# A second Strassen step for four of the seven products of V in layer 1 of two attention blocks

## The chip, the cores and the metric

The kernel runs on one core of one Trainium2 chip. The metric is the time of one execution on the device in microseconds; the median of three runs is given, and one execution was profiled.

## The reference

Two attention blocks follow each other on x of 8 images, 512 channels and 32 x 32 = 1024 positions, all in float32. Layer 0 has a group norm, 8 heads and a residual. Layer 1, which the change is about, normalises a whole image and has one head over all channels. Cut to what matters:

```python
n = (x - mean) * rsqrt(var + EPS) * gn_gamma + gn_beta      # mean, var over an image
q, k, v = wq @ n + bq, wk @ n + bk, wv @ n + bv             # 512 x 512 weights, 1024 positions
attn = softmax(q.T @ k * c ** -0.5)                         # 1024 x 1024
x = x + wo @ (v @ attn.T) + bo
```

## The kernel before

The program is unrolled over the 8 images. For each one it runs `layer0` (V, the last q and k, attention by pairs of heads, the projection, and at its end the first q and k of the next image) and then `attention1` (q, V, scores, values). The orders of TensorE, ScalarE and VectorE are those in which the program is written (`manual_schedule`). The DMA queue of SyncE (SP below) and GpSimd (POOL) are ordered by the framework, which also adds the waits.

**Folded weights.** Layer 1 multiplies wq with wk and wv with wo once, at the start. So `attention1` makes one product for q (`wqk1`), uses x itself in the place of k, and one product for V (`wvo1`), after whose use in the values no projection is left. V here means `wvo1` times x.

**Strassen.** Nearly every product is done in Winograd's form of Strassen's scheme: the two operands are cut into quarters A11 to A22 and B11 to B22, and seven products of quarters and of their sums S1 to S4 and T1 to T4 replace eight. Three of the seven, A11 B11, S2 T2 and S3 T3, are summed up one after the other in one bank of PSUM, together with A22 T4 (the generator `strassen` calls it `line`); ScalarE copies the running sum out after each of the first three, and VectorE adds the other bank (`single`) to the copies.

**Layer 1's V before** is `make_v` at L648 for both halves of the positions, with the products in `by_positions` at L617. A product of quarters has 4 matmul calls for each half: two blocks of 128 positions are the stationary operand, the 256 channels of the weight are the moving one, and 256 input channels are summed in two calls. In the profile a call leaves two records of TensorE (PE) and two of its weight load (PEld), here and everywhere.

**The second step** is there already in two places. The scores of layer 1 take it for four products in `twice` (L1267), with halves made by `halve_a` and `halve_b`. Layer 0's q and k take it in `by_two_steps` (L513): the products in `PAIRS`, namely A12 B21, S1 T1, S4 B22 and A22 T4, are each cut once more into seven, and two of them share a bank. The generator `pair(n)` makes one step for each of the seven inner products; the generator `line(i)` makes the three products that keep one step, and adds them to what the pairs left. `together` goes round its generators, one step each, so `pair(0)` and `pair(1)` alternate for 14 steps and `line(0)` and `line(1)` for 6. `WeightTwice` (L483) holds the inner sums of a weight's four parts: it makes them once, stores them in DRAM, and loads them for each image as two tiles of 512 KB.

**Order.** `at_steps(steps, {n: [...]})` runs the hooks of n after step n was issued. Because the engines take the order of the program, a hook's instructions stand on VectorE between the sums of step n and those of step n + 1. Before the change, `attention1` has these hooks:

```python
at_steps(together(make_q(0), make_q(1)), {..., 6: halve_b("T1"), 7: halve_b("B22"), ...})   # q
at_steps(together(*[make_v(...) for n2 in range(2)]), {                                      # V
    1: [finish_q], 4: [lambda: halve_a("S1")], 6: [lambda: halve_a("A12")],
    8: [lambda: halve_a("S4")],
})
at_steps(together(line(0), p5, line(1), p5), {})                                             # scores
at_steps(together(line(2), p2, line(3), p2), {..., 4: halve_a("A22"), 6: halve_b("T4"), ...})
```

`finish_q` makes S1 to S4 of q with `finish` (L187 to L190), four sums of 128x1024 at once. `halve_a` is L468 and `halve_b` L477 in the profile, four sums of 128x256 each.

**Buffers.** Nearly all tiles of 128x1024 come from one pool of 36 (`tile2`). PSUM has two tags, "s" and "o", with two tiles of two banks each. Weights rotate through three tiles; `next_weight` takes the next one and issues the load of the one after the next on SP's queue (L208).

Of the kernel before, what the change touches and what calls it, by code (L numbers as in the profile page):

```python
# [39 lines left out]
ALU = mybir.AluOpType  # L40
# [6 lines left out]
P = 128  # L47
# [3 lines left out]
NT = N // P  # L51
# [14 lines left out]
def two_attention_blocks(  # L66
# [34 lines left out]
    def tile2(name):  # L101
        return tpool.tile([P, 2, HALF], FP, tag="t", name=name)
# [80 lines left out]
        t = t.rearrange("p (a k o) -> p a k o", a=len(A_PARTS), o=width)  # L183
        return {a: t[:, n, :, :] for n, a in enumerate(A_PARTS)}

    def finish(parts, a21):
        nc.vector.tensor_tensor(parts["S1"], a21, parts["A22"], ALU.add)  # L187
        nc.vector.tensor_tensor(parts["S2"], parts["S1"], parts["A11"], ALU.subtract)
        nc.vector.tensor_tensor(parts["S3"], parts["A11"], a21, ALU.subtract)
        nc.vector.tensor_tensor(parts["S4"], parts["A12"], parts["S2"], ALU.subtract)  # L190

    W_SIZE = len(A_PARTS) * C
    stored = {}
# [65 lines left out]
    def next_weight():  # L259

        w = waiting.pop(0)
        if coming:
            name = coming.pop(0)
            waiting.append(Weight(name) if name in stored else load_first(name))
        return w
# [34 lines left out]
    class Norm:  # L300
# [54 lines left out]
        def bias(self):  # L355
            both, bias = self.tile("both"), self.tile("bias", NC)
            nc.vector.tensor_tensor(both, self.mean, self.rstd, ALU.mult)
            nc.vector.tensor_scalar(bias, made["v_g"], both, None, ALU.mult)
            nc.vector.tensor_tensor(bias, made["v_b"], bias, ALU.subtract)
            return bias  # L360
# [149 lines left out]
                    made[a] = q  # L510
            return made

    def by_two_steps(rows_of, twice_a, bs, twice_b, pairs, bias, name):  # L513

        def pair(n):
            line, single = (banks(tag, f"ps_{tag}{n}_{name}")[:, 0, :] for tag in "so")  # L520

            def multiply(bank, x, y, start):
                for i, (a, v) in enumerate(PAIRS[n]):
                    nc.tensor.matmul(  # L524
                        bank[:, i * 2 * P : (i + 1) * 2 * P], twice_a[a][x], twice_b[v][y],
                        start=start and i == 0, stop=True, skip_group_check=True,
                    )

            def at(r, t):
                return pairs[n][r][:, :, t * 2 * P : (t + 1) * 2 * P]  # L530

            def of(bank):
                return bank.rearrange("p (i q) -> p i q", i=2)

            def add(bank, r, t):
                nc.vector.tensor_tensor(at(r, t), of(bank), at(r, t), ALU.add)

            def take(bank, r, t):
                nc.scalar.copy(at(r, t), of(bank))

            for bank, x, y, start, use, r, t in [
                (line, "A11", "B11", True, take, 0, 0), (single, "A12", "B21", True, add, 0, 0),
                (line, "S2", "T2", False, take, 0, 1), (single, "S1", "T1", True, take, 1, 1),
                (line, "S3", "T3", False, add, 1, 1), (single, "S4", "B22", False, add, 0, 1),
                (line, "A22", "T4", False, take, 1, 0),
            ]:
                multiply(bank, x, y, start)
                use(bank, r, t)
                yield

        def line(i):
            bank = banks("o", f"ps_l{i}_{name}")[:, 0, :]

            def multiply(a, v, start):
                for k in range(2):
                    nc.tensor.matmul(  # L556
                        bank, rows_of(i, a)[:, k, :], bs[v][:, k, :], start=start and k == 0,
                        stop=k == 1, skip_group_check=True,
                    )

            def add(j, half, n):
                c = pairs[j][i][:, half, :]
                nc.vector.scalar_tensor_tensor(c, bank, bias(i, n), c, ALU.add, ALU.add)

            (c11, c22), (c12, _) = ([p[i][:, half, :] for half in range(2)] for p in pairs)
            nc.vector.tensor_tensor(c12, c12, c22, ALU.add)
            multiply("A11", "B11", True)
            add(0, 0, 0)
            yield
            multiply("S2", "T2", False)  # L570
            add(1, 0, 0)
            yield
            multiply("S3", "T3", False)
            add(0, 1, 1)
            add(1, 1, 1)
            yield

        yield from together(pair(0), pair(1))
        yield from together(line(0), line(1))

# [16 lines left out]
    def at_steps(steps, hooks):  # L597

        n = -1
        for n, _ in enumerate(steps):  # L600
            for hook in hooks.get(n, []):
                hook()
        assert n >= max(hooks, default=-1)
# [199 lines left out]
    def blank(n, name):  # L803
        return [tile2(f"{name}_{i}") for i in range(n)]

    def flat(t):
        return t.rearrange("p h n -> p (h n)")
# [15 lines left out]
    def pairs_qk_twice(w, twice_a, oc, bs, twice_b, qs, ks, b):  # L823

        pairs = [[tile2(f"{n}_{name}_0_{b}_{oc}") for name in "qk"] for n in ["c11", "c12"]]
        for i, ts in enumerate([qs, ks]):
            (c11, c22), (c12, c21) = ([p[i][:, half, :] for half in range(2)] for p in pairs)
            ts[oc], ts[oc + 2] = [c11, c12], [c21, c22]

        def bias(i, n):  # L830
            at = [V_BQ0, V_BK0][i] + oc + 2 * n
            return vec[:, at : at + 1]

        of = both_of(w)
        return by_two_steps(of, twice_a.all(of), bs, twice_b, pairs, bias, f"qk_0_{b}")

    ORDER = [0, 2, 1, 3]

# [321 lines left out]
    def attention1(xs, norm, b, at_values):  # L1160
# [9 lines left out]

        qs = quarters_of(f"q_1_{b}")
        w = next_weight().parts[0]
        combine, later = Combined(f"1_{b}"), []
        combine.take(xs)
        bs = combine.parts
# [8 lines left out]
        def halve_b(name):  # L1184
            twice_b[name] = quarters_b(bs[name], f"{name}_twice_{b}")

        def make_q(c):
# [24 lines left out]
            4: [norm.deviation, lambda: combine.make(4)],  # L1212
            6: [lambda: halve_b("T1")],
            7: [lambda: halve_b("B22")],
            5: [norm.untaken, lambda: later.pop(0)(), lambda: later.pop(0)()],
        })
        bias = norm.bias()
        vs = blank(NT // 2, f"v_1_{b}")
        w = next_weight().parts[0]
        (a11, a21), (a12, a22) = qs  # L1220
        q_parts = {"A11": a11, "A12": a12, "A22": a22}

        def finish_q():
            for i in range(1, 5):
                q_parts[f"S{i}"] = tile2(f"s{i}_q_{b}")
            finish(q_parts, a21)

        at_steps(together(*[make_v(w, n2, bs, vs, f"v_1_{b}") for n2 in range(2)]), {
            1: [finish_q], 4: [lambda: halve_a("S1")], 6: [lambda: halve_a("A12")],
            8: [lambda: halve_a("S4")],  # L1230
        })


# [97 lines left out]
        def c22(k):  # L1331
# [1 line left out]
            exp_of(ps[1][k][1])  # L1333

        p5 = twice("S1", "T1", "oo", 1, 1, True, False)
        at_steps(together(line(0), p5, line(1), p5), {})
        p2 = twice("A12", "B21", "oo", 0, 0, False, True)
        at_steps(together(line(2), p2, line(3), p2), {
            0: [lambda: with_p5(0, 1, 0)], 1: [lambda: c22(0)], 4: [lambda: halve_a("A22")],
            6: [lambda: halve_b("T4")], 8: [lambda: with_p5(0, 1, 1)], 10: [lambda: add_up(1, 0, 1)],  # L1340
        })
        at_steps(together(
            twice("S4", "B22", "so", 0, 1, False, True), twice("A22", "T4", "so", 1, 0, False, True)
# [1 line left out]

        tps = {f"T{n}": [tile2(f"t{n}_p_1_{b}_{k}") for k in range(2)] for n in range(1, 5)}
        svs = {f"S{n}": tile2(f"s{n}_v_1_{b}") for n in range(1, 5)}
        v_parts = [
            {
                "A11": vs[k][:, :, : 2 * P], "A12": vs[2 + k][:, :, : 2 * P],  # L1350
                "A22": vs[2 + k][:, :, 2 * P :],
                **{n: flat(t).rearrange("p (h u o) -> p h u o", h=2, u=2)[:, k] for n, t in svs.items()},
            }
            for k in range(2)
# [9 lines left out]
        def finish_values(n):  # L1364

            for k in range(2):
                a, b, a21, b12 = v_parts[k], p_parts[k], vs[k][:, :, 2 * P :], ps[0][k][1]
                x, y, op = {
                    1: (a21, a["A22"], ALU.add), 2: (a["S1"], a["A11"], ALU.subtract),
                    3: (a["A11"], a21, ALU.subtract), 4: (a["A12"], a["S2"], ALU.subtract),  # L1370
                }[n]
                nc.vector.tensor_tensor(a[f"S{n}"], x, y, op)
                x, y = {
                    1: (b12, b["B11"]), 2: (b["B22"], b["T1"]), 3: (b["B22"], b12), 4: (b["B21"], b["T2"]),
                }[n]
                nc.vector.tensor_tensor(b[f"T{n}"], x, y, ALU.subtract)
# [107 lines left out]
    with tc.manual_schedule(engines={PE, ACT, DVE}):  # L1484
# [41 lines left out]
        def channels_of(half, ccs):  # L1526
# [21 lines left out]
        w = next_weight()  # L1548
        at_steps(together(*pairs_qk(w, 0, combine.parts, qs, ks, 0)), {
            1: [lambda: combine.make(2), wvo1.finish], 2: [through_q, lambda: combine.make(3)],  # L1550
            4: [lambda: combine.make(4)], 7: [wqk1.finish], 8: [waiting[0].finish],
        })
        bs = combine.parts
        for rows in throughs:
# [432 lines left out]
```

## Time and profile before

| | us |
|---|---|
| median of 3 runs (2861.86 to 2862.79) | 2862.69 |
| the profiled execution | 2861.29 |
| its span, from the first to the last instruction | 2859.6 |
| TensorE busy in the span | 2852.0 |
| VectorE busy | 2020.6 |
| ScalarE busy | 1110.3 |
| layer 1's V on TensorE, one image (8 of them) | 24.17 |

The span is covered by the profile; what lies around it is the rest of the execution's time. In the page, a row of an engine gives its busy time, its share of the span and its instructions. In the rows of groups, `a x512 | 113.1, 379` is the number of records, the busy time of all together and the mean length in ns of one. Records of TensorE overlap, because each one's end is modelled with the time until its result is out; so what a record costs in a stream is read from start to start, or from a piece of the chain of waits divided by its records. The clock that TensorE was granted stands as full in every slice.

### The profile page before, as it was taken

What the parts mean: (1) busy time and instruction counts of PE and PEld (TensorE: products, weight loads), DVE (VectorE), ACT (ScalarE), POOL (GpSimd) and SP (SyncE); (2) the same over time, 40 slices, a digit from 0 to 9 for tenths busy, and PEclk for the clock granted to TensorE, in tenths of its full rate; (3) what the DMA queues carried; (4) which work ended last, traced back from release to release, by engine and by line L of the source; (5) the groups of instructions that cost most, each with busy time, mean ns of one, the idle gap of its engine ahead of it and who ended that gap; (6) DMA issues with size and microseconds to landing.
All of it is one profiled execution on the core that took longest, in us unless ns stands there. A gap on an engine that the chain in (4) does not pass through costs nothing.

```text
span 2859.6 us, 36447 instructions
## 1 busy us (share of the span) xinstructions
PE 2852.0 (100%) x14648; PEld 1468.0 (51%) x14648; DVE 2020.6 (71%) x2722; ACT 1110.3 (39%) x1536; POOL 109.5 (4%) x84
## 2 busy tenths in 40 slices
PE   9999999999999999999999999999999999999999
PEld 5434655347543475434663356633566335563365
DVE  5686586865867658776677766777667776667857
ACT  3462324623256231552325523255232652326432
POOL 0000010000000010000100001000010000100001
PEclk9999999999999999999999999999999999999999
DMA  8512132121322213212042120421204222121001
GB/s 273 177 42 74 52 110 93 42 74 52 111 93 49 69 49 114 93 46 92 26 136 72 44 92 26 136 78 45 85 26 136 79 55 77 38 99 65 8 1 38
DMA packets 79969, 219.31 MB, mean 77 GB/s; under 512 B 20144, under 2 KB 20912, under 8 KB 73392
## 3 DMA queue, kind: packets, MB, share of 16 engines
q1 hardware_dynamic: 79648, 216.87, 23.8%
q8 instruction: 117, 1.92, 0.3%
q14 instruction: 60, 0.49, 0.1%
q10 hardware_dynamic: 144, 0.02, 0.0%
HBM read 144.77 MB, written 29.62 MB: 61 GB/s over the span
## 4 chain that ended last, share of the span: by engine, by line
PE 98%; DVE 1%; SPq 0%; DMA 0%; issue 0%; ACT 0%; POOL 0%; DVEq 0%; POOLq 0%
PE s L872 16%; PE ps_o L891 15%; PE ps_v L625 14%; PE ps_o L1384 13%; PE ps_q L610 10%; PE ps_p L610 6%; PE ps_s L1260 6%; PE ps_l L1276 4%; PE ps_k L610 3%; PE ps_s L1276 3%; PE ps_l_qk L556 3%; PE ps_s_qk L524 2%; PE ps_o_qk L524 1%; PE ps_wvo L727 1%; PE ps_wqk L757 0%; PE ps_o L1441 0%
## 5 line engine op out<-in xcount | busy, mean ns | idle before, releaser
L776 ACT ACTIVATE p<-s 128x1024 f32<-128x1024 f32 x512 | 523.9, 1025 | 322.1 <-PE s L872 309.7
L778 DVE TENSOR_TENSOR acc<-acc,p 128x1024 f32<-128x1024 f32 x384 | 469.1, 1222 | 99.1 <-ACT p L776 86.0
L891 PE MATMUL ps_o<-p,v 64*64 64x512 f32 x4096 | 528.7, 589 | 0.0
L891 PEld LDWEIGHTS ps_o<-p,v 64*64 64x64 f32 x4096 | 156.6, 133 | 282.8 <-issue 278.6
L872 PE MATMUL s<-q,k 64*64 64x512 f32 x2304 | 298.5, 591 | 0.0
L872 PE MATMUL s<-c_q,c_k 64*64 64x512 f32 x1792 | 233.0, 590 | 0.0
L421 ACT COPY u_v<-ps_v 128x512 f32<-128x512 f32 x96 | 56.3, 586 | 304.9 <-PE ps_v L625 252.0
L872 PEld LDWEIGHTS s<-q,k 64*64 64x64 f32 x2304 | 86.3, 133 | 162.6 <-issue 156.6
L1384 PE MATMUL ps_o<-t_p,s_v 128*128 128x512 f32 x384 | 168.2, 594 | 0.0
L659 DVE TENSOR_TENSOR v<-ps_v,u_v 128x512 f32<-128x512 f32 x96 | 66.2, 689 | 142.1 <-PE ps_v L625 101.2
L872 PEld LDWEIGHTS s<-c_q,c_k 64*64 64x64 f32 x1792 | 67.7, 133 | 126.3 <-issue 114.9
L778 DVE TENSOR_TENSOR acc<-p,p 128x1024 f32<-128x1024 f32 x64 | 77.8, 1216 | 73.9 <-ACT p L776 73.9
L1286 DVE TENSOR_TENSOR p<-ps_l,p 128x512 f32<-128x512 f32 x104 | 71.1, 690 | 82.0 <-PE ps_l L1276 82.0
L1384 PEld LDWEIGHTS ps_o<-t_p,s_v 128*128 128x128 f32 x384 | 72.3, 190 | 94.5 <-issue 87.1
L1260 PE MATMUL ps_s<-s_q,t 128*128 128x512 f32 x256 | 120.3, 592 | 0.0
L1249 ACT ACTIVATE p<-p,factor 128x512 f32<-128x512 f32 (+1 forms) x112 | 86.8, 782 | 77.4 <-DVE p L1286 50.3
L610 PE MATMUL ps_q<-t,w_wqk 128*128 128x512 f32 x256 | 116.0, 597 | 0.0
L610 PE MATMUL ps_p<-t_p,w_p 128*128 128x512 f32 x256 | 114.5, 596 | 0.7 <-DVE inv L789 0.5
L1286 DVE TENSOR_TENSOR p<-ps_s,p 128x512 f32<-128x512 f32 x88 | 60.7, 689 | 75.0 <-PE ps_s L1276 74.2
L625 PE MATMUL ps_v<-w_wvo,t 128*128 128x256 f32 x512 | 113.1, 379 | 0.0
L421 ACT COPY u_q<-ps_q 128x512 f32<-128x512 f32 x75 | 43.6, 581 | 177.1 <-PE ps_q L610 177.1
L1384 PE MATMUL ps_o<-p,v 128*128 128x512 f32 x256 | 111.8, 594 | 0.1
(366 smaller groups left out, 4386.0 us busy)
## 6 DMA issues: line engine op xcount, KB each, us to landing
x<-in_x SPq DMA_DIRECT2D x92, 512.0 KB, 7.1
w_qk<-stored_qk SPq DMA_DIRECT2D x14, 1792.0 KB, 7.4
inv<-inv SPq DMA_DIRECT2D x248, 64.0 KB, 2.0
w_wqk<-stored_wqk SPq DMA_DIRECT2D x8, 1792.0 KB, 7.7
fold<-acc SPq DMA_DIRECT2D x56, 256.0 KB, 3.1
w_wvo<-stored_wvo SPq DMA_DIRECT2D x8, 1792.0 KB, 7.6
out<-x SPq DMA_DIRECT2D x28, 512.0 KB, 2.8
w_v<-stored_v SPq DMA_DIRECT2D x7, 1792.0 KB, 7.0
```

The lines of the kernel that those rows point to most:

```text
L421: nc.scalar.copy(us[n][:, :width], line[:, :width])
L610: nc.tensor.matmul(bank, w[a][:, k, c * P : (c + 1) * P], bs[b][:, k, :], start=fresh and k == 0, stop=k == 1, skip_group_check=True,)
L625: nc.tensor.matmul(bank[:, u * 2 * P : (u + 1) * 2 * P], bs[b][:, k, n * P : (n + 1) * P], w[a][:, k, :], start=fresh and u == k == 0, sto ...
L776: nc.scalar.activation(p, s, AF.Exp, scale=factor)
L778: nc.vector.tensor_tensor(acc, first, p, ALU.add)
L872: nc.tensor.matmul(s[cols, j, :], ks[pair][k0 // HALF][rows, k0 % HALF : k0 % HALF + HD], qs[pair][g][rows, :], start=True, stop=True,)
L891: nc.tensor.matmul(o[cols, half, :], vs[kt][rows, c0 : c0 + HD], p[rows, j, :], start=kt == 0, stop=kt == NT - 1,)
L1249: nc.scalar.activation(p, p, AF.Exp, scale=norm.factor)
L1260: nc.tensor.matmul(bank, bs[v][:, k, t * P : (t + 1) * P], q_parts[a][:, k, :], start=a == "A11" and k == 0, stop=k == 1, skip_group_check ...
L1276: nc.tensor.matmul(bank[:, u * 2 * P : (u + 1) * 2 * P], v[y][:, u * P : (u + 1) * P], a[x], start=start and u == 0, stop=True, skip_group ...
L1286: nc.vector.tensor_tensor(at(r, t), bank, at(r, t), ALU.add)
L1384: nc.tensor.matmul(bank, v_parts[kt // 2][a][:, kt % 2, c * P : (c + 1) * P], p_parts[kt // 2][b][:, kt % 2, cols], start=fresh and kt == ...
```

## The change

- Layer 1's V is made by `by_two_steps` in place of two `make_v`. The three products of the lines keep their form. The four products of `PAIRS` are cut once more, into pieces with 128 positions as the stationary operand, 128 channels as the moving one and 128 input channels summed in one call; a step of a pair has 4 calls.
- `by_two_steps` takes the matmuls, the places of the results and the bias as arguments, so that layer 0 and layer 1 share it. Layer 0's instructions stay as they were.
- The inner sums of `wvo1` are made once, at step 5 of the first q and k (16 sums of 128x128), stored, and loaded at the start of each `attention1`.
- V's results lie in four tiles in another arrangement (`v_pairs`); the values read them through `quarter_v`.
- q's sums S1 to S4 are made one by one after steps 5, 7, 9 and 11 of V. `halve_a("S1")` goes to step 13 of V, `halve_a("A12")` and `halve_a("S4")` go to steps 4 and 8 of the first stage of the scores, and `halve_b("T4")` goes from the second stage of the scores to step 8 of q.

The core of the diff:

```diff
-    def by_two_steps(rows_of, twice_a, bs, twice_b, pairs, bias, name):
+    def by_two_steps(multiply, multiply_line, pairs, at, bias, name):
...
-            def add(j, half, n):
-                c = pairs[j][i][:, half, :]
-                nc.vector.scalar_tensor_tensor(c, bank, bias(i, n), c, ALU.add, ALU.add)
+            def add(n, half, of):
+                c = pairs[n][i][:, half, :]
+                if bias is None:
+                    nc.vector.tensor_tensor(c, bank, c, ALU.add)
+                else:
+                    nc.vector.scalar_tensor_tensor(c, bank, bias(i, of), c, ALU.add, ALU.add)
...
+    def columns_of(w):
+        return lambda i, name: w.parts[0][name][:, :, i * P : (i + 1) * P]
+
+    def make_v_twice(w, twice_a, bs, twice_b, pairs, name):
+        parts = twice_a.all(columns_of(w))
+
+        def multiply(bank, n, x, y, start):
+            for i, (a, v) in enumerate(PAIRS[n]):
+                for u in range(2):
+                    nc.tensor.matmul(
+                        bank[:, (2 * i + u) * P : (2 * i + u + 1) * P],
+                        twice_b[v][y][:, u * P : (u + 1) * P], parts[a][x],
+                        start=start and i == u == 0, stop=True, skip_group_check=True,
+                    )
+
+        def multiply_line(i, bank, a, v, start):
+            by_positions(w.parts[0], i, bs)(bank, a, v, start)
+
+        def at(n, r, t):
+            both = flat(pairs[n][t]).rearrange("p (m o) -> p m o", m=4)
+            return both[:, :, r * P : (r + 1) * P]
+
+        return by_two_steps(multiply, multiply_line, pairs, at, None, name)
...
         w = next_weight().parts[0]
+        twice_w = WeightTwice("wvo1")
...
             7: [lambda: halve_b("B22")],
+            8: [lambda: halve_b("T4")],
...
-        at_steps(together(*[make_v(w, n2, bs, vs, f"v_1_{b}") for n2 in range(2)]), {
-            1: [finish_q], 4: [lambda: halve_a("S1")], 6: [lambda: halve_a("A12")],
-            8: [lambda: halve_a("S4")],
+        def finish_q(n):
+            q_parts[f"S{n}"] = tile2(f"s{n}_q_{b}")
+            finish(q_parts, a21, n)
+
+        at_steps(make_v_twice(w, twice_w, bs, twice_b, v_pairs, f"v_1_{b}"), {
+            **{2 * n + 3: [lambda n=n: finish_q(n)] for n in range(1, 5)}, 13: [lambda: halve_a("S1")],
         })
...
-        at_steps(together(line(0), p5, line(1), p5), {})
+        at_steps(together(line(0), p5, line(1), p5), {
+            4: [lambda: halve_a("A12")], 8: [lambda: halve_a("S4")],
+        })
...
-            6: [lambda: halve_b("T4")], 8: [lambda: with_p5(0, 1, 1)], 10: [lambda: add_up(1, 0, 1)],
+            8: [lambda: with_p5(0, 1, 1)], 10: [lambda: add_up(1, 0, 1)],
...
-            4: [lambda: combine.make(4)], 7: [wqk1.finish], 8: [waiting[0].finish],
+            4: [lambda: combine.make(4)], 5: [lambda: WeightTwice("wvo1", columns_of(wvo1))],
+            7: [wqk1.finish], 8: [waiting[0].finish],
```

More of the change, by code (lines that the diff above doesn't have):

```diff
@@ L184, in parts_of, with finish @@
         return {a: t[:, n, :, :] for n, a in enumerate(A_PARTS)}
[L186 to L190, printed above, removed]
+    def finish(parts, a21, n=None):
+        of = {**parts, "A21": a21}
+        for i, x, y, op in [
+            (1, "A21", "A22", ALU.add), (2, "S1", "A11", ALU.subtract),
+            (3, "A11", "A21", ALU.subtract), (4, "A12", "S2", ALU.subtract),
+        ]:
+            if n in (None, i):
+                nc.vector.tensor_tensor(parts[f"S{i}"], of[x], of[y], op)
     W_SIZE = len(A_PARTS) * C
@@ L511, in all, with of, add, take @@
             return made
-    def by_two_steps(rows_of, twice_a, bs, twice_b, pairs, bias, name):
+    def by_two_steps(multiply, multiply_line, pairs, at, bias, name):
         def pair(n):
             line, single = (banks(tag, f"ps_{tag}{n}_{name}")[:, 0, :] for tag in "so")
[L522 to L539, printed above, removed]
+            def of(bank, to):
+                return bank.rearrange("p (i q) -> p i q", i=to.shape[1])
+            def add(bank, to):
+                nc.vector.tensor_tensor(to, of(bank, to), to, ALU.add)
+            def take(bank, to):
+                nc.scalar.copy(to, of(bank, to))
             for bank, x, y, start, use, r, t in [
@@ L546, in pair @@
             ]:
-                multiply(bank, x, y, start)
-                use(bank, r, t)
+                multiply(bank, n, x, y, start)
+                use(bank, at(n, r, t))
                 yield
@@ L552, in line @@
             bank = banks("o", f"ps_l{i}_{name}")[:, 0, :]
[L554 to L559, printed above, removed]
-            def add(j, half, n):
-                c = pairs[j][i][:, half, :]
-                nc.vector.scalar_tensor_tensor(c, bank, bias(i, n), c, ALU.add, ALU.add)
+            def add(n, half, of):
[4 more added lines that the diff above has]
+                    nc.vector.scalar_tensor_tensor(c, bank, bias(i, of), c, ALU.add, ALU.add)
             (c11, c22), (c12, _) = ([p[i][:, half, :] for half in range(2)] for p in pairs)
             nc.vector.tensor_tensor(c12, c12, c22, ALU.add)
-            multiply("A11", "B11", True)
+            multiply_line(i, bank, "A11", "B11", True)
             add(0, 0, 0)
             yield
-            multiply("S2", "T2", False)
+            multiply_line(i, bank, "S2", "T2", False)
             add(1, 0, 0)
             yield
-            multiply("S3", "T3", False)
+            multiply_line(i, bank, "S3", "T3", False)
             add(0, 1, 1)
@@ L834, in pairs_qk_twice, with multiply, multiply_line, at @@
         of = both_of(w)
-        return by_two_steps(of, twice_a.all(of), bs, twice_b, pairs, bias, f"qk_0_{b}")
+        parts = twice_a.all(of)
+        def multiply(bank, n, x, y, start):
+            for i, (a, v) in enumerate(PAIRS[n]):
+                nc.tensor.matmul(
+                    bank[:, i * 2 * P : (i + 1) * 2 * P], parts[a][x], twice_b[v][y],
+                    start=start and i == 0, stop=True, skip_group_check=True,
+                )
+        def multiply_line(i, bank, a, v, start):
+            for k in range(2):
+                nc.tensor.matmul(
+                    bank, of(i, a)[:, k, :], bs[v][:, k, :], start=start and k == 0, stop=k == 1,
+                    skip_group_check=True,
+                )
+        def at(n, r, t):
+            return pairs[n][r][:, :, t * 2 * P : (t + 1) * 2 * P]
+        return by_two_steps(multiply, multiply_line, pairs, at, bias, f"qk_0_{b}")
+    def columns_of(w):
+        return lambda i, name: w.parts[0][name][:, :, i * P : (i + 1) * P]
+    def make_v_twice(w, twice_a, bs, twice_b, pairs, name):
+        parts = twice_a.all(columns_of(w))
+        def multiply(bank, n, x, y, start):
+            for i, (a, v) in enumerate(PAIRS[n]):
+                for u in range(2):
+                    nc.tensor.matmul(
+                        bank[:, (2 * i + u) * P : (2 * i + u + 1) * P],
+                        twice_b[v][y][:, u * P : (u + 1) * P], parts[a][x],
+                        start=start and i == u == 0, stop=True, skip_group_check=True,
+                    )
+        def multiply_line(i, bank, a, v, start):
+            by_positions(w.parts[0], i, bs)(bank, a, v, start)
+        def at(n, r, t):
+            both = flat(pairs[n][t]).rearrange("p (m o) -> p m o", m=4)
+            return both[:, :, r * P : (r + 1) * P]
+        return by_two_steps(multiply, multiply_line, pairs, at, None, name)
     ORDER = [0, 2, 1, 3]
@@ L1217, in attention1 @@
         bias = norm.bias()
-        vs = blank(NT // 2, f"v_1_{b}")
-        w = next_weight().parts[0]
+        v_pairs = [[tile2(f"{n}_v_1_{b}_{k}") for k in range(2)] for n in ["c11", "c12"]]
+        w = next_weight()
         (a11, a21), (a12, a22) = qs
         q_parts = {"A11": a11, "A12": a12, "A22": a22}
[L1223 to L1226, printed above, removed]
-        at_steps(together(*[make_v(w, n2, bs, vs, f"v_1_{b}") for n2 in range(2)]), {
-            1: [finish_q], 4: [lambda: halve_a("S1")], 6: [lambda: halve_a("A12")],
-            8: [lambda: halve_a("S4")],
+        def finish_q(n):
[3 more added lines that the diff above has]
+            **{2 * n + 3: [lambda n=n: finish_q(n)] for n in range(1, 5)}, 13: [lambda: halve_a("S1")],
         })
@@ L1347, in attention1 @@
         svs = {f"S{n}": tile2(f"s{n}_v_1_{b}") for n in range(1, 5)}
+        quarter_v = [
+            [[flat(t)[:, i * HALF : (i + 1) * HALF].rearrange("p (u o) -> p u o", u=2) for t in pair]
+             for i in range(2)] for pair in v_pairs
+        ]
         v_parts = [
             {
-                "A11": vs[k][:, :, : 2 * P], "A12": vs[2 + k][:, :, : 2 * P],
-                "A22": vs[2 + k][:, :, 2 * P :],
+                "A11": quarter_v[0][0][k], "A12": quarter_v[1][0][k], "A22": quarter_v[0][1][k],
                 **{n: flat(t).rearrange("p (h u o) -> p h u o", h=2, u=2)[:, k] for n, t in svs.items()},
@@ L1366, in finish_values @@
             for k in range(2):
-                a, b, a21, b12 = v_parts[k], p_parts[k], vs[k][:, :, 2 * P :], ps[0][k][1]
+                a, b, a21, b12 = v_parts[k], p_parts[k], quarter_v[1][1][k], ps[0][k][1]
                 x, y, op = {
```

## The prediction

> **What bounds the kernel now.** I read the page's engine shares first, then the chain of waits around one V of layer 1 (image 1, 647 to 672 us), then the windows of that stretch, then VectorE's timeline inside it, and last the records that tell what a matmul of 128 columns costs, because none stands in the page.
>
> ```profile
> PE 2852.0 (100%) x14648; PEld 1468.0 (51%) x14648; DVE 2020.6 (71%) x2722; ACT 1110.3 (39%) x1536; POOL 109.5 (4%) x84
> ...
> 647.41 24.17 PE ps_v L625 x112
> ...
> 647.40:671.60 24.20, 24.20 (x114) 21.31 (x113) 13.43 (x25) 5.50 (x9) 0.00 (x0) 1.00 0.22 77
> ```
>
> TensorE is never idle, and 98% of the chain is its own. So the time falls only where TensorE's work does. Layer 1's V is 24.17 us for 112 records in all eight images. A matmul call of the program leaves two records (896 records of `ps_v<-w_wvo` for 448 calls), so one record of 256 columns costs 24.17/112 = 0.2158 us, and one of 512 costs 0.429 us (17.41 us for 40 records, with a small wait, at `ps_o` L1384). VectorE has 13.43 us in 24.20 and ScalarE 5.50: neither binds here today.
>
> **TensorE's saving.** Today V is 7 products x 8 calls x 256 columns. Afterwards three products stay as they are (both `line` groups: 2 x 3 steps x 4 calls = 24 calls, 48 records): 48 x 0.2158 = 10.36 us. The other four become `pair(0)` and `pair(1)`: 14 steps of 4 calls with 128 columns, 56 calls, 112 records. By columns alone these are 7/8 of the old work; what one such record costs decides everything. The break-even is (24.17 - 10.36)/112 = 0.1233 us.
>
> ```profile
> 1.58 2.55 PE L1491 MATMUL ps_warm<-in_sample 128*128 128x128 f32 x11
> ...
> 1.59 2.47 PEld L1491 LDWEIGHTS ps_warm<-in_sample 128*128 128x128 f32 x11
> ...
> 6.40 0.34 PEld L727 LDWEIGHTS ps_wvo<-wo,nv 128*128 128x128 f32 x1 [0.52 <-issue]
> ...
> 7.42 0.19 PEld L727 LDWEIGHTS ps_wvo<-wo,nv 128*128 128x128 f32 x1 [0.24 <-issue]
> 7.85 0.19 PEld L727 LDWEIGHTS ps_wvo<-wo,nv 128*128 128x128 f32 x1 [0.24 <-issue]
> ...
> 452.35 0.19 PEld L285 LDWEIGHTS ps_m<-stat,in_group 128*128 128x128 f32 x1 [0.24 <-issue]
> 452.46 0.30 PEld L556 LDWEIGHTS ps_l_qk<-x,w_qk 128*128 128x128 f32 x2
> ```
>
> The only stream of this shape is the warm-up. Eleven loads and eleven matmuls of 128 columns run in it side by side: (2.55 - 0.42)/10 = 0.213 us from one matmul to the next, and (2.47 - 0.333)/10 = 0.214 from load to load. That is before TensorE reached its pace: at 5.54 and 6.40 us the same loads stand 0.86 us apart, at 7.42 and 7.85 they stand 0.43 apart. Half of 0.213 is 0.107. At full pace the load itself sets a floor: behind a matmul of 4 columns the next load follows 0.11 us later (452.35, 452.46; and the two in the last row take 0.30 = 0.19 + 0.11). So a record of 128 columns costs from 0.107 (columns) to 0.112 (load); I take 0.111: 112 x 0.111 = 12.43 us. V's TensorE work is 22.79 us, **1.38 us less per image**.
>
> A rule of the Trainium skill speaks against it: TensorE: Matmul & The Clock Gate, section Back-to-back issue gap, says that in a stream of load and matmul pairs the spacing is set by both, and gives about 81 ns for 128 columns where a matmul alone has 56. At that ratio of 1.45 a record would cost 0.161 us, V 10.36 + 18.0 = 28.4, and the kernel 8 x 4.2 = 34 us more. The warm-up rows show the maximum of the two and no surcharge, and the page's 131 ns for 512 columns does not fit the 0.429 us here either. I go with the rows and keep the rule as the slow rival.
>
> **VectorE.** Today V has 6 sums out of PSUM; afterwards 6 in the pairs and 10 in the lines (two `c12 + c22`, eight adds of a bank; the third line product goes to two tiles). ScalarE keeps 8 copies (0.586 us each, x96 and x32 in the page's rows of `ps_v`). The moves: q's four sums go from V's step 1 to steps 5, 7, 9, 11; S1's halves from step 4 to 13; A12 and S4 into the first stage of the scores, T4 from the second stage of the scores to q's step 8.
>
> ```profile
> 657.42 1.22 DVE L189 TENSOR_TENSOR s_q<-q,q 128x1024 f32<-128x1024 f32 x1
> 658.56 1.22 DVE L190 TENSOR_TENSOR s_q<-q,s_q 128x1024 f32<-128x1024 f32 x1
> 659.69 0.42 DVE L468 TENSOR_TENSOR S_twice<-s_q 128x256 f32<-128x256 f32 x1
> 660.15 0.42 DVE L468 TENSOR_TENSOR S_twice<-S_twice,s_q 128x256 f32<-128x256 f32 x1
> ...
> 684.59 0.69 DVE L1286 TENSOR_TENSOR p<-ps_l,p 128x512 f32<-128x512 f32 x1 [7.05 <-PE ps_l L1276]
> ...
> PEld ps_l_qk L556 <- DVE c_q L563: 3.8, 6, 0.6
> ```
>
> From start to start a sum of 1024 takes 1.14 us, four of 256 take 1.47 (0.46 and three of 0.34), one of 512 takes 0.61. Pairs: 6 x 0.61 + 4 x 1.14 + 1.47 = 9.7 us in TensorE's 12.43; lines: 10 x 0.61 = 6.1 in 10.36. It fits on average; the order is what costs. A sum starts some 0.27 us after its matmuls' last slot (441.14 to 441.41 in the same form in layer 0). Counted from V's start, with 0.1 us for waits, step 9's sum starts at 9.3; then S3 to 11.05, the sums of steps 10 and 11 to 12.27, S4 to 13.4, S1's halves to 14.9, `c12 + c22` to 15.5, and only then line(0)'s first add, until 16.2. Step 16 accumulates into that bank and is due at about 16.0. A load that has not been fetched ahead costs a further 0.1, so TensorE waits some 0.3 us there; line(1) follows 1.7 us later and has time. The last row shows that the same form in layer 0 does wait for such an add (3.8 us in 6 waits). The lines' later adds end before their banks are wanted again, and the scores' first use of those banks comes 1.7 us after V.
>
> The other moves I cost at nothing, by what covers them. A12 and S4 (2 x 1.47) fall into VectorE's idle 7.05 us before 684.59 and the 4.54 before 676.85. T4's halves start after the sum of 644.0 and end at 646.2, before that of 647.45; if they did not, the last sum of q would be late by under 1.5 us, and nothing on TensorE wants it for 5 us. Taking T4 out of the second score stage gains nothing, since TensorE does not wait there. Should A12 be late, the first product of the second stage (from 688.6) would wait.
>
> **The weights' sums: DMA and the start.**
>
> ```profile
> 622.96 0.34 SPq L208 DMA_DIRECT2D w_v<-stored_v  x1
> 647.44 24.49 SPq L208 DMA_DIRECT2D w_qk<-stored_qk  x2
> ...
> qk_twice<-stored_qk_twice SPq DMA_DIRECT2D x14, 512.0 KB, 8.9
> ```
>
> Each image loads two tiles of 512 KB more, on SP's queue behind `w_v`. By the rows 623.0 + 7.0 + 8.9 = 639 us, 8 us before V at 647.4; SP has nothing else until 647.44. Two first waits for these tiles (as in layer 0, `EVENT_SEMAPHORE` of 51 ns) have no slack in a stream of 0.111 us: 0.1 us per image, between 0 and 0.2. The two tiles also take slots of the pool of 36; I find 35 or 36 alive at the fullest place in both kernels, so 0, with a late slot showing as a late load.
>
> Once, at the start, VectorE makes 16 sums of 128x128. Between rows of 256 and 512 each 256 columns cost 0.27 us, so 0.21 each and 0.11 for each dependent one: 3.7 us, in an idle stretch of VectorE from 48.2 to 52.7. Their two stores stand on SP beside the load of layer 0's V weights, which is issued at 53.35 and wanted at 58.3. 1 MB there could delay it by up to 4 us, of which TensorE would see 0 to 3; I take 0.5.
>
> **The sum.** 8 x (1.38 - 0.32 - 0.1) = 7.7, less 0.5: 7.2 us off. The profiled execution took 2861.29 us (span 2859.6), so 2854.1; it stands 1.4 us under the median of the three runs (2862.69), so against the median 2855.5. About 0.2%, 5.7 us, is what a measurement of this kernel can tell from no change, so the likeliest outcome is close to that line.
>
> **The rivals.**
> - *The load shows.* Place: the 112 records of 128 columns. It decides at 0.119 us per record with the waits above (0.123 without). At 0.161 the time is 2862.7 + 34 = 2897; at 0.125 it is 10.36 + 14.0 + 0.1 = 24.5, 2.4 us over 8 images, plus 0.5: 2866. For it: 128-column loads never ran back to back at full pace for long in this trace. Against: the 0.11 of 452.46 and the equal 0.213. 12%.
> - *VectorE takes the gain back.* If its sums with four strided blocks of 128 are slower than the 0.69 of the rows, or a second bank waits, each image loses 0.5 to 1 us more: 2859 to 2864. For it: the path in the steps 9 to 16 has no slack at all. Against: halved blocks of 256 in layer 0 take the same 0.69. 18%.
> - *More than I count.* Records at 0.108 and no wait: V is 22.5 us, 8 x 1.7 = 13.6 less: 2849. 8%.
> - *The forecast* has 62%: 2853 to 2858.
>
> The range 2850 to 2864 takes in the forecast, nearly all of the second rival and part of the others. Faster by over 0.2% (under 2857.0): 62% less its slow edge, plus the third rival, 0.66; the same 0.20; slower 0.14.
>
> **What would show it.** V's piece in the chain of waits at 23.0 to 23.4 us in place of 24.17, with 160 records; TensorE's instructions 14648 + 8 x 48 = 15032; a wait of the lines' loads for VectorE of about 0.3 us, eight times; loads of 128 columns 0.11 apart. Pairs above 13.3 us in V, or waits inside the pairs' steps, would make the forecast wrong; so would a V0 at the start that begins later than 60.6.

## The result, and the profile after

| | before | after |
|---|---|---|
| median of 8 runs, us | 2861.49 (2860.39 to 2862.79) | 2852.68 (2852.23 to 2853.40) |
| ratio after to before | | 0.9969 (95% interval 0.9958 to 0.9980) |
| profiled execution, us | 2861.29 | 2853.40 |
| its span, us | 2859.6 | 2851.7 |

The kernel became 8.8 us faster by the medians, where 7.2 were forecast, and 7.9 us by the two profiled executions, to which the sums below refer. The page's engine shares and its queues for instructions, after:

```profile
PE 2843.5 (100%) x15032; PEld 1470.1 (52%) x15032; DVE 2075.9 (73%) x2818; ACT 1108.4 (39%) x1536; POOL 109.4 (4%) x84
...
q8 instruction: 120, 1.97, 0.3%
q14 instruction: 62, 0.51, 0.1%
```

TensorE is as full as it was and has 8.5 us less to do, with 384 records more. VectorE has 55 us more, and no row of it stands in the chain of V. One short wait for it is left inside the last row, that of the lines. The chain of waits for image 1 after (start, length, what):

```profile
646.19 1.78 PE ps_s_v L859 x16
647.98 1.79 PE ps_o_v L859 x16
649.76 1.79 PE ps_s_v L859 x16
651.55 1.79 PE ps_o_v L859 x16
653.34 1.79 PE ps_s_v L859 x16
655.12 1.79 PE ps_o_v L859 x16
656.91 1.79 PE ps_s_v L859 x16
658.70 10.59 PE ps_l_v L617 x48
```

And the stretch of V after in windows: all of it, the pairs, the lines (after the length come the busy times of TensorE, its loads, VectorE, ScalarE and GpSimd):

```profile
646.00:669.10 23.10, 23.10 (x161) 21.55 (x160) 16.25 (x26) 5.29 (x9) 0.00 (x0) 1.00 0.21 81
646.00:658.50 12.50, 12.50 (x113) 12.47 (x112) 8.85 (x14) 4.70 (x8) 0.00 (x0) 1.00 0.39 149
658.50:669.10 10.60, 10.60 (x50) 9.08 (x50) 7.39 (x13) 0.59 (x1) 0.00 (x0) 1.00 0.00 0
```

Each piece of the pairs is two steps, 16 records of 128 columns in 1.79 us: 0.1117 us each. The pairs take 112 x 0.1117 = 12.51 us and the lines 10.58 (48 x 0.2158 = 10.36, and a wait of 0.22): V is 23.09 us where it was 24.17 (23.16 in image 2, where the wait is 0.29). In the pairs the loads are busy 12.47 of 12.50 us; before, they were busy 21.31 of 24.20 in V. From the first record of a stage to the first of the next, summed over the images:

| stage | before, us | after, us |
|---|---|---|
| q of layer 1 | 195.84 | 195.84 |
| V of layer 1 | 193.39 | 184.80 |
| scores | 359.58 | 359.58 |
| values | 394.82 | 394.81 |
| projection of layer 0 | 196.64 | 197.84 |
| V, q and k, attention of layer 0 | 1479.09 | 1479.08 |

The chain and the stages agree: V gave 8.6 us, the projections took 1.2 back, and the rest of the difference in span, 0.5 us, lies before the first and after the last stage. Those stretches vary by as much between profiles in which their code is the same: from the first matmul to the first projection `before` has 245.94 us and `moves_only` (below) 245.09, and from the start of the last values to the end of the span the runs with the change have 54.90 to 55.54.

### The profile page after: what moved, and what is told of

It reads as the page before. It is cut to its first block, busy times and chain, and to the rows that moved or that the text cites. A ratio compares the mean times of both kernels' runs of the same rounds, so it can differ in the third digit from the quotient of the medians.

```text
span 2851.7 us, 37404 instructions
## 1 busy us (share of the span) xinstructions
PE 2843.5 (100%) x15032; PEld 1470.1 (52%) x15032; DVE 2075.9 (73%) x2818; ACT 1108.4 (39%) x1536; POOL 109.4 (4%) x84
## 4 chain that ended last, share of the span: by engine, by line
PE 97%; DVE 2%; DMA 1%; SPq 1%; issue 0%; ACT 0%; POOL 0%; DVEq 0%; ACTq 0%; POOLq 0%
PE s L909 15%; PE ps_o L928 15%; PE ps_o L1427 13%; PE ps_q L602 10%; PE ps_v L617 7%; PE ps_s L1298 6%; PE ps_p L602 6%; PE ps_l L1314 4%; PE ps_k L602 3%; PE ps_l_v L617 3%; PE ps_s L1314 3%; PE ps_l_qk L838 3%; PE ps_s_v L859 2%; PE ps_s_qk L831 2%; PE ps_o_v L859 2%; PE ps_o_qk L831 1%
## 5 line engine op out<-in xcount | busy, mean ns | idle before, releaser
L1302 ACT COPY p<-ps_s 128x512 f32<-128x512 f32 x96 | 56.1, 585 | 196.9 <-PE ps_s L1298 195.8
L1427 PE MATMUL ps_o<-p,c_v 128*128 128x512 f32 x256 | 111.8, 594 | 0.1
L1054 DVE RECIPROCAL inv<-inv 128x512 f32<-128x512 f32 x28 | 93.7, 3346 | 22.9 <-ACT inv L777 22.9
L425 ACT COPY u_v<-ps_v 128x512 f32<-128x512 f32 x48 | 28.1, 586 | 201.7 <-PE ps_v L617 157.5
```

Of the source, the lines that this page charges most:

```text
L1054: nc.vector.reciprocal(invs[g], invs[g])
L1427: nc.tensor.matmul(bank, v_parts[kt // 2][a][:, kt % 2, c * P : (c + 1) * P], p_parts[kt // 2][b][:, kt % 2, cols], start=fresh and kt == ...
```

## The experiments

**1. What sets a record of 128 columns.** Run `cols64`; every call of the pairs became two of 64 columns, with the same operands and results:

```diff
                 for u in range(2):
-                    nc.tensor.matmul(bank[:, (2 * i + u) * P : ...], twice_b..., parts[a][x], ...)
+                    for h in range(2):
+                        nc.tensor.matmul(bank[:, at0 : at0 + HD], twice_b..., parts[a][x][:, h * HD : (h + 1) * HD], ...)
```

> The changed kernel with every call of the pairs split into two of 64 columns, same operands, same results: 224 records of 64 columns in place of 112 of 128 per image. It measures what sets the 0.1117 us of a record of 128 columns. Theory (the load sets it): a record of 64 columns costs the same 0.11, V is 224 x 0.1117 + 10.36 = 35.4 us, the kernel 98 us more (about 2951). Rival (the columns set it, and the load is hidden behind them): a record of 64 costs half, 0.055, V stays about 23, and the time is about 2853. Rule of the back-to-back section (both add up in part): a record between the two, 0.08 to 0.1, V 28 to 33.

The chain of waits of this run, around V of image 1:

```profile
661.22 3.57 PE ps_o_v L861 x32
664.79 3.57 PE ps_s_v L861 x32
668.37 3.57 PE ps_o_v L861 x32
671.94 3.57 PE ps_s_v L861 x32
```

3.57/32 = 0.1116 us: half the columns cost the same. V is 35.37 us in every image and the execution 2950.17 (one run), as the theory of the load has it. One rival is not in the expectation: the rate at which TensorE can start instructions at all. The trace after the change has a row against it, in which eight loads of a narrower tile, 128x32, take 0.16 us together:

```profile
42.86 0.16 PEld L679 LDWEIGHTS ps_q<-nk,many_bias_q 128*32 128x32 f32 x8 [0.76 <-issue]
```

So a load of 128x128 in float32, 0.1117 us from one to the next, is the floor of the records of 64 and 128 columns here, and the columns run behind it unseen. The rule that load and columns add up in part does not hold for this shape in float32. The break-even with the wait as it came out (0.22 us) is (24.17 - 10.58)/112 = 0.1213 us, 9% above the record's cost.

**2. The wait at the lines, and the order on VectorE.** Run `s1_later`:

```diff
-            ..., 13: [lambda: halve_a("S1")],
+            ..., 15: [lambda: halve_a("S1")],
```

> The changed kernel with one edit: S1's halves after step 15 of V in place of step 13, so that they stand on VectorE behind the first adds of both lines. Theory (order on VectorE): the lines' first add comes 1.47 us earlier, step 16 finds its bank free, and V falls from 23.09 to 22.87 us in every image, 1.8 us for the kernel (2851); no load of the lines waits for VectorE. Rival (the wait at step 16 has another cause, such as the bank's change of tile or a weight that is read late): V stays at 23.09, and the load at step 16 still waits. Second rival (S1's halves are now late for the scores): V falls, but the scores' 44.95 us grow by as much.

VectorE's timeline after, at the seam of pairs and lines, with the load's row under it:

```profile
658.17 1.22 DVE L194 TENSOR_TENSOR s_q<-q,s_q 128x1024 f32<-128x1024 f32 x1
659.30 0.42 DVE L472 TENSOR_TENSOR S_twice<-s_q 128x256 f32<-128x256 f32 x1
...
660.77 0.69 DVE L558 TENSOR_TENSOR c_v<-c_v,c_v 128x512 f32<-128x512 f32 x1
661.37 0.68 DVE L553 TENSOR_TENSOR c_v<-ps_l_v,c_v 128x512 f32<-128x512 f32 x1
...
662.11 6.77 PEld L617 LDWEIGHTS ps_l_v<-w_wvo,t 128*128 128x128 f32 x32 [0.36 <-DVE c_v L553]
```

The first add of the lines starts at 661.37, 2.67 us after the lines began in the chain (658.70); it ends at 662.05, and the load of step 16 follows at 662.11. In `s1_later` VectorE's row for the same add, and the lines' piece of the chain of waits:

```profile
660.00 0.69 DVE L553 TENSOR_TENSOR c_v<-ps_l_v,c_v 128x512 f32<-128x512 f32 x1 [0.42 <-PE ps_l_v L617]
```

```profile
658.23 10.36 PE ps_l_v L617 x48
```

The add starts 1.77 us after the lines' beginning: it waits for TensorE and not the reverse, the lines take 48 x 0.2158 = 10.36 us, V is 22.87 in all eight images, and the scores keep 44.95. No load of the lines waits for VectorE any more. The median is 2851.89 (before on that chip 2861.93; ratio 0.9964, 0.9950 to 0.9977). The 1.8 us show in the stages of the trace; the projections are 0.6 us longer in this profile (198.5 in all), and the intervals of the two ratios overlap, so the times alone would not tell the two kernels apart.

**3. What dealing the sums out is worth.** Run `not_dealt`:

```diff
-            **{2 * n + 3: [lambda n=n: finish_q(n)] for n in range(1, 5)}, 13: [lambda: halve_a("S1")],
+            1: [lambda n=n: finish_q(n) for n in range(1, 5)], 4: [lambda: halve_a("S1")],
+            6: [lambda: halve_a("A12")], 8: [lambda: halve_a("S4")],
...
-            4: [lambda: halve_a("A12")], 8: [lambda: halve_a("S4")],
```

> The changed kernel with V's hooks as they were before: q's four sums together after step 1 of V, the halves of S1, A12 and S4 after steps 4, 6 and 8, none in the scores; T4's halves stay in q, since V needs them. Theory (order on VectorE): the four sums end about 6.3 us after V's start, the two adds of steps 2 and 3 wait behind them until 7.5, and step 6 of the pairs, due at 5.4, waits for its bank until about 7.1; from there TensorE keeps its lead. V is 22.87 + 1.8 = 24.6 us, more than the 24.17 of before: the kernel takes about 2865 us, 12 more than the changed one, and the gain is gone. Rival (VectorE's lag is taken up by the two banks of each tag, because it has idle time on average): V within 0.3 us of 23.09, about 2853.

The timeline of VectorE and of TensorE's loads in V of image 1, and the wait in the list of waits (total in us, times, longest):

```profile
652.73 1.22 DVE L194 TENSOR_TENSOR s_q<-q,s_q 128x1024 f32<-128x1024 f32 x1
653.87 1.28 DVE L532 TENSOR_TENSOR c_v<-ps_o_v,c_v 128x512 f32<-128x512 f32 x2
...
654.61 0.52 PEld L859 LDWEIGHTS ps_o_v<-wvo_twice,B_twice 128*128 128x128 f32 x4 [1.85 <-DVE c_v L532]
```

```profile
PEld ps_o_v L859 <- DVE c_v L532: 14.8, 8, 1.9
```

The two adds of steps 2 and 3 stand behind the four sums until 653.87; step 6 gets its bank at 654.61, 1.85 us late, in each of the eight images (14.8 us). V is 24.80 us, 0.2 more than expected and 0.63 more than before the change. The median is 2867.15, and the ratio to before 1.0019 (1.0012 to 1.0026). With the old order of the sums the kernel is 5.2 us slower than before the change, by the medians: the second Strassen step is worth its 8.6 us only with the sums dealt out.

**4. The moves by themselves.** Run `moves_only`, the kernel before with the new places of q's sums and halves (steps 2 to 5 and 6 of V, which has 10 steps there) and V by one step:

> The kernel before with the moves alone: V by one step of Strassen as it was, q's sums one by one after steps 2 to 5 of V, S1's halves after step 6, A12 and S4 in the scores' first stage, T4's halves in q. Theory (the gain is TensorE's work in V): V stays 24.17 us, scores 44.95, values 49.35, time within 1 us of before. Rival (part of the gain comes from the moves, by a VectorE that is less behind when the scores or the values begin): 2 to 4 us less than before, seen in the scores or values.

V 24.17 us, scores 44.95, values 49.35, median 2861.54 against 2861.93: ratio 0.9998 (0.9990 to 1.0006). By themselves the moves bring nothing; they only make room for the second step.

**5. Where the projections' 1.2 us went.** In the stages two projections stand out: image 6, 25.34 us after and 24.26 before, and image 3, 24.84 and 24.30. Images 2 and 5 became shorter, from 24.62 and 24.50 to 24.33 and 24.35. The chain of waits after, in image 6:

```profile
2345.07 4.78 DMA wvo_twice<-stored_wvo_twice
2349.85 0.03 issue
2349.88 3.02 DMA inv<-inv
2352.90 0.03 issue
2352.92 0.05 DVEq L948
2352.97 0.04 issue
2353.02 0.69 DVE o L948
```

SP's queue there:

```profile
2339.69 4.98 SPq L1060 DMA_DIRECT2D inv<-inv  x8
2345.07 0.35 SPq L495 DMA_DIRECT2D wvo_twice<-stored_wvo_twice  x1
2345.53 5.92 SPq L1060 DMA_DIRECT2D inv<-inv  x8
```

The first of the two new loads had been put on SP's queue among the 16 small copies that spread the softmax's inverses, and not behind `w_v`, as the prediction had it. The chain runs through it, so it was the first suspect. Run `load_later`, with run `both` (this edit and that of `s1_later`):

```diff
-        twice_w = WeightTwice("wvo1")
+        twice_w = []
...
-            2: [norm.mean_of_all, lambda: combine.make(3)],
+            2: [norm.mean_of_all, lambda: combine.make(3), lambda: twice_w.append(WeightTwice("wvo1"))],
```

> The changed kernel with the load of the weights' inner sums written as a hook of q's step 2 in place of the start of attention1, which puts both loads on SP's queue behind the load of w_v and out of the 16 small copies of the softmax's inverses at the end of layer 0. Theory (the load of 512 KB that now stands among those copies makes the last inverse late): the projection of image 6 goes from 25.34 to about 24.3 us and the others stay at 24.2 to 24.6, about 1.2 us less in all; V keeps its 23.09, since the loads land by about 12 us into q, 12 before V. Rival (the projection's time is chance from run to run): image 6 stays above 25. Second rival (a load from q's step 2 is too late): V's first pair steps wait for it.

The expectation failed. Both loads went behind `w_v`, V kept its 23.09 us, and image 6 still took 24.98 us, image 3 24.78; the median is 2852.87 (ratio 0.9968, 0.9956 to 0.9980). Nor does the load's place go with the delay in the changed kernel: it stands between the eighth and the ninth copy in all of the first seven, and images 0, 1, 2, 4 and 5 take 24.24 to 24.35. So the load's place is not what makes images 3 and 6 late, although the chain named it.

> The changed kernel with both edits, S1's halves after step 15 of V and the loads behind w_v. Theory: V 22.87 us and the projections as before, so 8 x 1.30 = 10.4 us less than the kernel before: about 2851.3 against 2861.9, and 1.8 + 1.2 less than the changed kernel. Rival (the two edits meet: VectorE or SP takes one of them back): between 2852 and 2853.

V 22.87 us, median 2850.36 against 2862.05: ratio 0.9962 (0.9948 to 0.9975). This is the lowest median of all. The order on VectorE gives V its 1.8 us in it. Image 6 is still at 25.21, but image 3 is at 24.29, and all projections together take 197.0 us against 198.5 in `s1_later`; whether the moved loads have a part in that is not shown.

**6. The other suspect, the fetch of instructions.** The queues in the DMA view of the 13 us around the late copy, image 6 (packets, MB, share of the DMA engines). Before, 2346 to 2359 us:

```profile
q1 hardware_dynamic: 783, 1.26, 44.2%
```

After, 2340 to 2353 us:

```profile
q1 hardware_dynamic: 924, 1.75, 56.2%
q8 instruction: 1, 0.02, 0.6%
q14 instruction: 1, 0.01, 0.2%
```

A packet of 16 KB of an instruction queue lies there after and does not before. The page has 120 such packets on q8 for TensorE's 2 x 15032 matmuls and loads, one in about 250 (before the change 117 for 2 x 14648), so q8 is taken to be TensorE's, and the packets' place against the stages moves when instructions are added. Runs `shift188` and `shift208` are `both` with 47 and 52 calls of 4 columns more in the warm-up:

```diff
             nc.tensor.matmul(warm, in_sample, in_sample, start=True, stop=True)
+        for n in range(47):
+            nc.tensor.matmul(warm[:, :4], in_sample, in_sample[:, :4], start=True, stop=True)
```

> The kernel of run both with 47 further calls of 4 columns in the warm-up at the start: 188 more instructions of TensorE ahead of everything, and nothing else. They cost 94 records of 0.11 to 0.21 us, 10 to 20 us, at the start. What is tested: the projection of image 6 was 25.2 us in both and 25.3 in the changed kernel, where the kernel before has 24.3, and in each of these profiles a packet of 16 KB of the queue for instructions lies in the 3 us in which the last inverses of the softmax are copied. These packets come once in 256 instructions of TensorE. Theory (the fetch of instructions makes the copy late): with a shift of 188, no packet falls between 9 us before and 3 us after the start of any of the first seven projections, and all seven take 24.2 to 24.4 us, image 6 too. Rival (image 6 has another cause, or chance): it stays above 25.

> The same with 52 calls, 208 instructions. Theory (the fetch of instructions makes the copy late): packets fall 0.4 us after the start of the projections of images 0 and 5, and of no other of the first seven; those two take 24.8 to 25.5 us, image 6 goes to 24.3. Rival (another cause, or chance): image 6 stays above 25, and images 0 and 5 at 24.3.

| | both | shift188 | shift208 |
|---|---|---|---|
| projection of image 0, us | 24.27 | 24.83 | 25.31 |
| image 2 | 24.34 | 24.76 | 24.33 |
| image 5 | 24.26 | 24.27 | 24.27 |
| image 6 | 25.21 | 24.33 | 24.34 |
| q8 packet within 10 us of the projection's start | images 3, 6: -6.0, +0.4 | images 0, 2, 5: +0.1, -6.3, -4.8 | images 0, 3, 5: -2.0, +2.3, -6.5 |

The DMA view of image 6 in `shift188` (2360 to 2373 us) has no packet of q8:

```profile
q1 hardware_dynamic: 783, 1.26, 42.8%
q14 instruction: 1, 0.01, 0.2%
```

VectorE's last division by the inverses for image 6, in the timeline of `both`, whose projection starts at 2346.2, and then in that of `shift188`, whose projection starts at 2369.8:

```profile
2349.89 0.69 DVE L948 TENSOR_TENSOR o<-o,inv 128x512 f32<-128x512 f32 x1 [2.13 <-DMA inv<-inv]
```

```profile
2372.62 0.69 DVE L948 TENSOR_TENSOR o<-o,inv 128x512 f32<-128x512 f32 x1 [1.24 <-DMA inv<-inv]
```

3.7 us after the start have become 2.8. Image 6 is late in all six runs with a second step in V and no shift (24.98 to 25.47) and quick in both shifted runs, so it was neither chance nor something about that image. The packet of q14 stands 6.0 us ahead of image 6 in `both` and in the two shifted runs alike, so it is q8's that made the difference. The late projections went where the packets went: to images 0 and 2, and to image 0. The exact places were not met: the packets are not spaced evenly, in `shift188` three lay near projections where none was expected, and image 5 was not late in `shift208`.

Over all ten profiles (one a run) and the first seven images the picture is the same (packets from 10 us before the projection's start to 4 after it):

| packets there | cases | projection, us |
|---|---|---|
| none | 43 | 24.23 to 24.36 |
| one of q14 alone | 6 | 24.33 to 24.62 |
| one of q8, 2.0 us before the start to 1.0 after | 7 | 24.83 to 25.47 |
| one of q8, 4.8 to 6.6 us before | 11 | 24.27 to 25.31; 4 of them below 24.30 |
| one of q8, 2.3 to 2.4 us after | 3 | 24.30 to 24.32 |

The last copy ends 2.33 to 2.35 us after the start without a packet, and up to 3.47 with one of q8. Image 3 of the changed kernel belongs to the fourth row (6.0 us before), and `both` has its packet at the same place and is quick, so for image 3 the cause is less certain than for image 6. That the fetch and the copies meet is shown; how the one holds up the other is not. The whole executions of these two, 2873.07 and 2871.99 us, carry the added warm-up of some 22 us and say nothing else.

## Why the prediction was right, and which terms were off

The forecast was 2855.5 us for the kernel and 7.2 us for the gain. The profile has a gain of 7.9. The kernel's median, 2852.68, lies in the range of 2850 to 2864 and 0.3 us below the likeliest band of 2853 to 2858; 1.2 of the 2.8 us that part it from 2855.5 come from the median before, 2862.69 over three runs and 2861.49 over eight. The mechanism came as forecast: less work on TensorE, and one wait for VectorE at step 16. That the total came so close is in part luck: two terms that were feared did not come (8 x 0.1 and 0.5 us), and one that nobody had (1.2 us) did. Term by term:

- **The record of 128 columns**, forecast 0.111 between 0.107 and 0.112: 0.1117 measured, from the load, as run `cols64` shows. The gain of TensorE's work per image is 24.17 - 10.36 - 12.51 = 1.30 in place of 1.38. The deciding number could be read before the change, from two loads behind a matmul of 4 columns and from the warm-up.
- **The slow rival**, built on the rule of the Trainium skill, TensorE: Matmul & The Clock Gate, section Back-to-back issue gap, needed more than 0.119 us per record. It did not come; by the section LDWEIGHTS of the same page, columns divided by 1.2, an estimate for this load is 107 ns, and the traces have 111.7 from load to load.
- **The wait of step 16**, forecast 0.32 for the chain S3, two adds, S4, S1's halves, `c12 + c22`, add: 0.22 measured at that very step in seven images and 0.29 in image 2, by those very instructions. It shows in two gaps between starts, 0.337 and 0.320 us where the stream has 0.216; the excess of the second, 0.10, fits the load that the forecast had as not fetched ahead. The forecast chain ended 16.2 us after V's start; the last of it ended at 662.05 - 646.03 = 16.0. VectorE's 0.69 held for the strided blocks too (0.687 to 0.691), so the second rival did not come, but `not_dealt` shows that it stood close: without the dealing out its mechanism costs 1.85 us per image.
- **The first waits for the two tiles**, forecast 0.1: no record of the pairs is late there. The two `EVENT_SEMAPHORE` stand in V's steps 1 and 2 in all images, and the matmuls beside them keep the pace of 0.112.
- **The start**, forecast 0.5 for a late load of layer 0's V weights: VectorE did wait 0.61 us for `w_v` before 58.82, and TensorE saw nothing; V of layer 0 began at 60.47 where it had begun at 60.63.
- **SP's queue** was the step that failed. The two loads did not stand behind `w_v`; one stood among the copies of the inverses. The place was costed at nothing, and five images with the load there are at most 0.06 us longer than before.
- **The projections** had no term, and took 1.2 us. In image 6 (1.1 us) the delay went with a packet of TensorE's instructions, whose place moves with the instructions that the change adds; for image 3 (0.5 us) the same is likely and not shown, and images 2 and 5 gave 0.4 us back.

So 8 x (1.30 - 0.22) = 8.6, less 1.2 for the projections, gives 7.4 of the 7.9; the 0.5 left lies at the start and the end and is within what these vary by between profiles.

## What to carry to other kernels

In a kernel that TensorE bounds without a gap, a second Strassen step pays by the record, not by the columns. Ask first what a stationary load costs back to back: where the columns of a record take less time than its load, as the 64 of `cols64` do, smaller pieces no longer save anything. Then write down the other engine's queue in the order in which it will run: VectorE had room on average in every version, and in `not_dealt` q's four sums ahead of two adds cost 14 us against the changed kernel, more than the whole gain. A new transfer in a chain of waits is a suspect, not a proof: move the transfer and look again.

## What the runs showed of the hardware that was not expected

- A record of 64 columns and one of 128 cost the same: 0.1116 and 0.1117 us, both the load's time (float32, load of 128x128, granted clock 1.00).
- A wait of its own on TensorE's queue (`EVENT_SEMAPHORE`, 51 ns) cost nothing in V, even in a stream of records 0.112 us apart.
- A fetch of 16 KB of TensorE's instructions near 16 copies of 64 KB went with a last copy up to 1.1 us later (3.47 against 2.33 us after the projection's start). Instructions added at the start of the kernel, in `shift188` and `shift208`, moved such a delay of about 1 us from one image to another.
